# Layer 1's queries and keys of a two-layer encoder: split into bf16 thirds before the transposition instead of after it, and transposed by DMAs, with a new set of ranks

## The chip, the core and the metric

The kernel runs on one core of a Trainium2 chip. The metric is the device time of one execution in microseconds (us). The kernel before was timed in three runs: 1556.82, 1558.4 and 1560.14 us, median 1558.4 us. The five engines run side by side and are named as in the profile: PE (TensorE, matmuls), DVE (VectorE), ACT (ScalarE), POOL (GpSimd) and SP (SyncE, which issues nearly all DMAs, in order).

## What is computed

Two encoder layers over x of 16 sequences, 512 tokens and 128 features, all in fp32, each with a residual and a normalisation without weights ahead of it:

```
x = x + L0_attn(layernorm(x))        # 16 heads of 8 features, biases on q, k, v
x = x + L0_ffn(layernorm(x))         # gated, hidden 384
x = x + L1_attn(layernorm(x))        # q = rms_norm(q) * qn_w, k = rms_norm(k) * kn_w, per head
x = x + L1_ffn(layernorm(x))         # base matmul plus gated low-rank experts

# both attentions, per sequence and head:
softmax((q @ k.T) / sqrt(8)) @ v
```

What matters for the change is layer 1's attention. Its q and k are normalised per head over their 8 features (`rms_norm`) and multiplied by a weight per feature (`qn_w`, `kn_w`), before the scores are formed.

## The kernel before, in words

**Units and tiles.** A unit is the attention of one sequence in one layer, with the feed-forward part behind it: 32 units, numbered n. The order is six units of layer 0, then layer 1 and layer 0 in turn, and six units of layer 1 at the end. A sequence lies in SBUF as 128 partitions by 4 blocks of 128 features ("tokens' rows"); after a transposition it is 128 features by 512 tokens ("features' rows").

**Scores in bf16 thirds.** An fp32 query is split into three bf16 parts that add up to it, and so is a key. Of the nine products six are formed at once: the parts are stacked along the contraction, six slots of 8 features for each head (`QPART`, `KPART`), in the tiles `qst` and `kst`, which exist three times (NST). One more slot, MSLOT, holds the row's maximum, itself split in three, so that the second product comes out with the maximum subtracted. The stacks are filled by DMAs, six copies for each tensor of a unit (L606), and for queries one more that clears MSLOT (L595).

**The three streams of a unit.** `maxima` forms all scores a first time (L777), pair by pair of 512 columns in PSUM, and DVE reduces each pair to the negated row maximum (L790). POOL splits a group's maxima (L813 to L820), a transposing DMA turns them (L824) and another puts them into the query stack (L827). `scores` forms the scores a second time, transposed (L847), and ACT takes the exponential (L861) into a ring of eight buffers. `values` multiplies by the values in fp32 into the bank `acc` (L878); ACT empties it (L895) into one of two `av` buffers, and SP stores that to DRAM (L901).

**Before and behind them.** `pre(n)` normalises the unit's input, transposes it (L548), and makes q, k and v. In layer 0, q and k come straight out of a product in features' rows. In layer 1 they come in tokens' rows (L656), since the norm of each head is a sum over 8 neighbours there: DVE adds the bias and sums squares, POOL runs three Newton steps for the inverse root (L695 to L701) and multiplies (L708, two halves). Then, for keys and for queries:

- PE transposes the four 128x128 blocks of the tensor, in fp32, into one PSUM bank (L726).
- `split_stack` (L560): ACT reads the bank twice, multiplying by the column of norm weights `qkn`, once into an fp32 tile t (L568) and once into the first bf16 third a1 (L570). POOL forms t - a1 (L575), rounds it to the second third a2 (L581), and forms the last one a3 (L585). For the first EARLY units DVE does this instead.
- SP issues the copies of a1, a2 and a3 into the stack (L606), each as soon as its third is there and the slot of unit n - 3 is free.

`post(n)` loads the weighted values and the denominators back (L944 to L956), multiplies by their inverse (L958), projects, and runs the feed-forward part.

**What sets the order.** The program is straight-line: `Plan` simulates the engines while the kernel is written, and picks for each engine what comes next. Each generator yields (engine, duration, rank, kind, what it waits for), and for a DMA also a pair of time until it lands and time that it occupies the DMA engines. On PE a score weighs kinds, ranks and the backlog of DVE and ACT (`choose`, L154); on the others the lowest rank wins among those that can start soon. The constants at the top (LEAD, VLAG, PAIR, AHEAD, UM, UB, LATE, PRE0, PRELEN, POST0, POSTLEN and so on) set the ranks and the booked times. LEAD is how many steps (16 steps to a unit) the maxima run ahead of the scores; PRE0 and PRELEN, POST0 and POSTLEN place the work of `pre` and `post` in steps. On the chip each engine runs its list in the order that was fixed this way, and each instruction waits for what it depends on; an instruction that waits holds up those behind it on its engine.

Of the kernel before, what the change touches and what calls it, by code (L numbers as in the profile page):

```python
# [10 lines left out]
F32 = mybir.dt.float32  # L11
BF16 = mybir.dt.bfloat16
# [36 lines left out]
LEAD = 20  # L49
NP = 8  # L50
VLAG = 3.35
# [19 lines left out]
SAME = 0.05  # L71
PRE0 = 0.03
PRELEN = 20.84
POST0 = 2.81
POSTLEN = 11.82
# [14 lines left out]
def act(n, ptr=0):  # L90
    return 51 + n / 1.2 + 93 * ptr


def dve(n):
    return 55 + n / 0.96
# [212 lines left out]
def encoder_kernel(ctx: ExitStack, tc: tile.TileContext, x, wf, wi, lb, cols, rows, out):  # L308
# [30 lines left out]
    r_t = ring("t", [P, S])  # L339
    r_qk = ring("qks", [P, C, 256], bufs=1)  # L340
# [51 lines left out]
    nc.vector.memset(busy.bitcast(F32), ONES)  # L392
    zero = const.tile([P, S], F32, name="zero")
# [5 lines left out]
    qkn = const.tile([P, 2], F32, name="qkn")  # L399
# [54 lines left out]
    def weights():  # L454
# [6 lines left out]
        nc.vector.tensor_scalar(qkn, cl[:, 2:4], math.sqrt(HD), None, ALU.mult)  # L461
# [12 lines left out]
        at["row2"] = t  # L474
        for k in range(3):
# [84 lines left out]
    def split_stack(pt, b, own, n, qk, layer, nm, tp, pr):  # L560

        if layer == 0:
            arg = dict(bias=cl[:, qk : qk + 1])
        else:
            arg = dict(scale=qkn[:, qk : qk + 1])
# [20 lines left out]
        r_t.give(kt, t)  # L586
        dst = (qst, kst)[qk][n % NST]
        part = (a1, a2, a3)
        avail = (ta, t2, t)
        stack = dst.rearrange("(x k) t s -> k x t s", k=8)  # L590
        end = t
# [17 lines left out]
        for rg, k in zip(r_a, (k1, k2, k3)):  # L609
            rg.give(k, end)  # L610
# [11 lines left out]
    def pre(n):  # L622
# [23 lines left out]
        if layer:  # L646
# [67 lines left out]
            r_ri.give(kri, t)  # L714
        for qk in (1, 0):
            if layer == 0:
                t = yield "PE", 860, pr(), "x", (tT, "w", banks.one, safe, r_t, r_a[0])
                b, pt = banks.take1()
                lo = (WQ0, WK0)[qk]
                product(pt, w[:, lo : lo + P], xT)  # L720
                tp = t
            else:
                tp = yield "PE", 440, pr(), "w", (t, banks.one, safe, r_t, r_a[0])
                b, pt = banks.take1()
                for c in range(C):
                    nc.tensor.transpose(  # L726
                        pt[:, c * P : (c + 1) * P], qk_sb[:, c, qk * P : (qk + 1) * P], ident
                    )
# [3 lines left out]
            plan.spawn(  # L732
                split_stack(pt, b, own, n, qk, layer, f"{qk}{nm}", tp, ramp(pr(), pr() + 3, 8))
            )
# [570 lines left out]
```

## Time and profile before

| | |
|---|---|
| profiled execution: its own time | 1556.45 us |
| its span, first to last instruction | 1554.7 us |
| mean granted TensorE clock | 0.998 |
| L790, DVE reduction of a pair, x1024 | 1208.7 us busy, 1217 ns each |
| L861, ACT exponential of a pair, x1024 | 1017.3 us, 1026 ns |
| L878, PE weighted values, x4096 | 546.6 us, 606 ns |
| L847 and L777, PE scores, x2048 each | 391.0 and 384.7 us, 382 and 381 ns |
| L726, PE transposes of layer 1's q and k, x128 | 21.3 us, 287 and 279 ns |
| L568 and L570, ACT evictions of layer 1's q and k, x64 | 44.1 us |
| L708, POOL normalisation, x32 | 40.2 us, 1276 ns |
| DMA engines, queue q1 (SP's) | 119.02 MB, 28.2% of 16 engines |

How to read it: times of matmuls are modelled and overlap, so a row's busy time on PE is more than the time that PE would save without it; the distance from one start to the next is the better measure. Share of the chain means the chain of work that ended last, followed back from the last instruction to what released it at each step. A wait is written "who, line <- what ended it: total us, times, longest". DMA issues are not counted as busy time of an engine; SP's queue shows for each how long the issue held it.

### The profile page before, as it was taken

The page shows a single profiled execution, that of the slowest core. Times are in us where ns is not written, and L with a number is a line of the kernel's source. Part 1 is how long each engine was busy: PE and PEld are TensorE (multiplying, and loading weights), DVE is VectorE, ACT ScalarE, POOL GpSimd, SP SyncE. Part 2 cuts the span into 40 slices and gives each one's busy share as a digit, 9 for nine tenths or more (in the row PEclk, how much of TensorE's full clock was granted, in tenths as well). Part 3 has the DMA queues.
Part 4 walks back from the last instruction along what each step waited for, and adds up shares of the span by engine and source line. Part 5 has one row for each costly group of instructions (what it writes and reads, how often), then busy time and mean ns, then how long its engine had stood idle before and what let it go on. Part 6 is the DMA issues. An engine that isn't in the chain of part 4 may idle for free.

```text
span 1554.7 us, 38057 instructions
## 1 busy us (share of the span) xinstructions
PE 1492.8 (96%) x14857; PEld 511.5 (33%) x14863; DVE 1453.6 (94%) x1941; ACT 1253.6 (81%) x1506; POOL 833.8 (54%) x1154
## 2 busy tenths in 40 slices
PE   8799999999999999999999999999999999999998
PEld 3222333333333323333333333323333332333223
DVE  6899999999999999999999999999999999999974
ACT  2688878888888888888888888888888888887784
POOL 5634346464464654737556473754647757475122
PEclk9999999999999999999999999999999999999999
DMA  5232223312333132333313333322333213233111
GB/s 138 65 97 72 61 66 89 84 45 75 85 104 83 57 93 69 98 82 98 84 48 84 87 98 83 82 76 66 91 84 92 81 48 85 81 90 97 47 54 39
DMA packets 133220, 122.83 MB, mean 79 GB/s; under 512 B 38660, under 2 KB 108388, under 8 KB 133040
## 3 DMA queue, kind: packets, MB, share of 16 engines
q1 hardware_dynamic: 132032, 119.02, 28.2%
q8 instruction: 116, 1.90, 0.5%
q10 hardware_dynamic: 1008, 1.38, 0.4%
q14 instruction: 64, 0.52, 0.1%
HBM read 23.43 MB, written 38.53 MB: 40 GB/s over the span
## 4 chain that ended last, share of the span: by engine, by line
PE 59%; DVE 25%; ACT 5%; issue 4%; POOL 3%; DMA 2%; SPq 1%; DVEq 0%; POOLq 0%; ACTq 0%
DVE nm L790 22%; PE acc L878 20%; PE pp L847 12%; PE pp L777 11%; PE one L450 10%; ACT p L861 3%; PE one L548 1%; PE one L1057 1%; PE acc L441 1%; PE one L726 1%; DMA rdb<-drd 1%; PE one L1043 1%; SPq L606 1%; ACT th_f L1047 1%; DVE th_f L1049 0%
## 5 line engine op out<-in xcount | busy, mean ns | idle before, releaser
L790 DVE TENSOR_REDUCE nm<-pp 128x2 f32<-128x1024 f32 x1024 | 1208.7, 1217 | 53.2 <-PE pp L777 35.4
L861 ACT ACTIVATE p<-pp 128x1024 f32<-128x1024 f32 x1024 | 1017.3, 1026 | 215.8 <-PE pp L847 193.6
L878 PE MATMUL acc<-p,vst 128*32 128x512 f32 x4096 | 546.6, 606 | 1.0 <-ACT av L895 0.2
L777 PE MATMUL pp<-kst,qst 64*128 64x512 bf16 x2048 | 384.7, 381 | 26.1 <-ACT p L861 11.3
L847 PE MATMUL pp<-qst,kst 64*128 64x512 bf16 x2048 | 391.0, 382 | 19.2 <-DVE nm L790 7.6
L847 PEld LDWEIGHTS <-kst 64*128 64x128 bf16 x2048 | 129.7, 93 | 401.5 <-issue 376.1
L777 PEld LDWEIGHTS <-qst 64*128 64x128 bf16 x2048 | 135.5, 94 | 319.8 <-issue 294.0
L878 PEld LDWEIGHTS acc<-p,vst 128*32 128x32 f32 x4096 | 83.4, 108 | 144.4 <-issue 130.1
L958 POOL TENSOR_TENSOR num<-num,rdb 128x512 f32<-128x512 f32 x31 | 39.5, 1275 | 116.7 <-DMA rdb<-drd 111.9
L895 ACT ACTIVATE av<-acc 128x512 f32<-128x512 f32 x128 | 77.1, 602 | 16.8 <-PE acc L878 14.9
L813 POOL CAST mp<-nm 128x32 bf16<-128x32 f32 x62 | 13.1, 211 | 138.8 <-DVE nm L790 138.8
L1068 POOL TENSOR_TENSOR h_f<-th_f,ub_f 128x512 f32<-128x512 f32 x32 | 40.8, 1276 | 82.9 <-ACT ub_f L1065 77.5
L450 PE MATMUL one<-w,xTa 128*32 128x128 f32 (+1 forms) x1392 | 63.2, 314 | 0.0
L556 POOL TENSOR_TENSOR xt<-xt,row 128x512 f32<-128x512 f32 x48 | 61.4, 1280 | 1.2 <-DVE xnf L510 1.2
L669 POOL TENSOR_TENSOR sq0a<-qksa 128x512 f32<-128x512 f32 x16 | 16.7, 1041 | 80.7 <-DVE qksa L663 61.4
L450 PE MATMUL one<-wd,h_f 128*32 128x128 f32 x1536 | 52.9, 276 | 0.3 <-DVE h_f L1072 0.3
L575 POOL TENSOR_TENSOR t1a<-t1a,a11a 128x512 f32<-128x512 f32 x31 | 36.0, 1161 | 21.3 <-ACT a11a L570 21.3
L450 PEld LDWEIGHTS one<-w,xTa 128*32 128x32 f32 x1392 | 36.9, 109 | 29.1 <-issue 17.1
L450 PEld LDWEIGHTS one<-wd,h_f 128*32 128x32 f32 x1536 | 38.7, 109 | 17.1 <-issue 15.2
L575 POOL TENSOR_TENSOR t0a<-t0a,a10a 128x512 f32<-128x512 f32 x31 | 36.0, 1160 | 10.3 <-ACT a10a L570 8.4
L708 POOL TENSOR_TENSOR qksa<-qksa,ria 128x512 f32<-128x512 f32 x32 | 40.2, 1276 | 1.3
L581 POOL TENSOR_TENSOR a21a<-t1a,zero 128x512 bf16<-128x512 f32 x31 | 39.6, 1277 | 2.4
(176 smaller groups left out, 1540.4 us busy)
## 6 DMA issues: line engine op xcount, KB each, us to landing
dav<-av SPq DMA_DIRECT2D x127, 256.0 KB
kst<-a11a SPq DMA_DIRECT2D x96, 128.0 KB
qst<-a10a SPq DMA_DIRECT2D x93, 128.0 KB
kst<-a21a SPq DMA_DIRECT2D x64, 128.0 KB
qst<-a20a SPq DMA_DIRECT2D x62, 128.0 KB
num<-dav SPq DMA_DIRECT2D x31, 256.0 KB
rdb<-drd SPq DMA_DIRECT2D x31, 256.0 KB
xt<-in_x_dram SPq DMA_DIRECT2D x16, 256.0 KB
```

Of the source, the lines that this page charges most:

```text
L450: nc.tensor.matmul(out[js], lhs[:, js], rhs, start=start, stop=stop, tile_position=(0, 32 * j))
L556: nc.gpsimd.tensor_tensor(xt, xt, row[:, None, lo : lo + P].to_broadcast([P, C, P]), ALU.add)
L575: eng.tensor_tensor(tt, tt, a1, ALU.subtract)
L581: nc.gpsimd.tensor_tensor(a2, tt, zero, ALU.add)
L708: nc.gpsimd.tensor_tensor(qkv4[:, gs], qkv4[:, gs], ri[:, gs, None, :].to_broadcast([P, 8, HD, 8]), ALU.mult,)
L777: nc.tensor.matmul(pt[:, k], qst[n % NST][band, t, qc * P : (qc + 1) * P], kst[n % NST][band, t], start=True, stop=True,)
L790: nc.vector.tensor_reduce(nm[:, :, t % T, qc] if half1 != half else nm[:, half, t % T, qc : qc + 2], pt, AX.X, ALU.max, negate=True,)
L847: nc.tensor.matmul(pair[:, half], kst[n % NST][band, t, kc * P : (kc + 1) * P], qst[n % NST][band, t], start=True, stop=True,)
L861: nc.scalar.activation(pt, pair, AF.Exp, scale=SCALE)
L878: nc.tensor.matmul(acc[32 * j : 32 * j + 32], vst[n % NST][:, kc, lo : lo + 32], p_of[n, i, kc, j // 2][0][:, j % 2], start=(kc == 0), sto ...
L895: nc.scalar.activation(av, acc, AF.Copy)
L1068: nc.gpsimd.tensor_tensor(h[:, f], th, ub, ALU.mult)
```

## The change

In layer 1, q and k stay in tokens' rows until they are in thirds. The norm weights become a row: a matrix of ones is multiplied by a diagonal of `qn_w * kn_w`, once at the start, so that every partition holds their product times 8, and POOL multiplies the queries by it (the keys are left as they are; the scores are the same). `split_tokens` then splits: ACT copies the tensor to the first bf16 third, POOL forms the remainder, rounds it to the second third (by adding zero) and forms the third one. Each third, 128 partitions by 512 bf16, is brought to features' rows by one transposing DMA on SP's queue. The stacking copies follow as before, now in `put_stack`. The PE transposes (L726), the two ACT evictions with scale and the PSUM bank they took are gone, and so is the rank that held this PE work back in layer 1 (`safe`). Layer 0 goes through `split_rows`, which is the old code. A ring of two buffers for each of the three thirds in tokens' rows is new. Nearly all ranks are set anew; EARLY is 2, so that unit 1 is split on DVE as well, and its first normalisation ends there.

```diff
-LEAD = 20
+LEAD = 19
-VLAG = 3.35
+VLAG = 2.04
...
-EARLY = 1
-MAXPR = 4.43
+EARLY = 2
+MAXPR = 9.8
-PAIR = 93.67
+PAIR = 13.08
+TRANS = (3000, 500)
-AHEAD = 447
+AHEAD = 555
-UM = {"m": 1.05, "e": 1.02, "v": 0.0, "x": -0.15, "w": -0.1}
-UB = {"m": 1652, "e": 1199}
-LATE = 10.81
-LATE_M = 7.9
-SAME = 0.05
-PRE0 = 0.03
+UM = {"m": 1.05, "e": 1.02, "v": 0.0, "x": -0.32, "w": -0.29}
+UB = {"m": 1660, "e": 1199}
+LATE = 7.7
+LATE_M = 2
+SAME = 0.02
+PRE0 = 3.16
-POST0 = 2.81
-POSTLEN = 11.82
+POST0 = 4.77
+POSTLEN = 20
...
+    r_b = [ring(f"b{k}", [P, C, P], BF16) for k in (1, 2, 3)]
...
-        nc.vector.tensor_scalar(qkn, cl[:, 2:4], math.sqrt(HD), None, ALU.mult)
...
+        t = yield "DVE", 300, -30, None, (r_rt, r_rt)
+        diag, kb = r_rt.take("diag")
+        nc.vector.tensor_scalar(diag, ident, cl[:, 2:3], cl[:, 3:4], ALU.mult, ALU.mult)
+        t = yield "PE", 224, -30, "x", (t, banks.one)
+        b, pt = banks.take1()
+        product(pt[:, :P], ones, diag)
+        r_rt.give(kb, t)
+        t = yield "DVE", dve(P), -30, None, (t,)
+        nc.vector.tensor_scalar(qkn, pt[:, :P], float(HD), None, ALU.mult)
...
+    def split_tokens(qk_sb, kq, n, qk, nm, t, pr):
+        x = qk_sb[:, :, qk * P : (qk + 1) * P]
+        z4 = zero.rearrange("p (c d) -> p c d", c=C)
+        parts, ks, avail = [], [], []
+        for k in range(3):
+            if k == 0:
+                t = yield "ACT", act(S), pr(), None, (t, r_b[0])
+                bt, kb = r_b[0].take(f"b0{nm}")
+                nc.scalar.activation(bt, x, AF.Copy)
+            else:
+                t = yield "POOL", 1180, pr(), None, (t, (r_t, r_b[2])[k - 1])
+                last = bt
+                if k == 1:
+                    tt, kt = r_t.take(f"t{nm}")
+                    tt = tt.rearrange("p (c d) -> p c d", c=C)
+                    nc.gpsimd.tensor_tensor(tt, x, last, ALU.subtract)
...
+                    nc.gpsimd.tensor_tensor(bt, tt, z4, ALU.add)
+                else:
...
+                    nc.gpsimd.tensor_tensor(bt, tt, last, ALU.subtract)
...
+            e = yield "SP", 600, pr(0.2), None, (t, r_a[k]), TRANS
+            a, ka = r_a[k].take(f"a{k}{nm}")
+            nc.sync.dma_start_transpose(
+                a.rearrange("p (c s) -> p c s", c=C), bt.rearrange("p c d -> p (c d)")
+            )
+            parts.append(a)
+            ks.append(ka)
+            avail.append(e)
+        r_b[2].give(kb, e)
+        yield from put_stack(parts, ks, avail, n, qk, pr)
...
+        if layer:
+            t = yield "POOL", 1280, pr(), None, (t - 80, "qkn")
+            q3 = qk_sb[:, :, :P]
+            nc.gpsimd.tensor_tensor(q3, q3, qkn[:, None, :].to_broadcast([P, C, P]), ALU.mult)
+            kq = [kq, 2]
         for qk in (1, 0):
-            if layer == 0:
-                t = yield "PE", 860, pr(), "x", (tT, "w", banks.one, safe, r_t, r_a[0])
...
-            else:
-                tp = yield "PE", 440, pr(), "w", (t, banks.one, safe, r_t, r_a[0])
-                b, pt = banks.take1()
-                for c in range(C):
-                    nc.tensor.transpose(
-                        pt[:, c * P : (c + 1) * P], qk_sb[:, c, qk * P : (qk + 1) * P], ident
-                    )
-                if qk == 0:
-                    r_qk.give(kq, tp)
+            ends = ramp(pr(), pr() + 3, 8)
+            if layer:
+                plan.spawn(split_tokens(qk_sb, kq, n, qk, f"{qk}{nm}", t, ends))
+                continue
+            t = yield "PE", 860, pr(), "x", (tT, "w", banks.one, safe, r_t, r_a[0])
```

More of the change, by code (lines that the diff above doesn't have):

```diff
@@ L392, in encoder_kernel @@
     nc.vector.memset(busy.bitcast(F32), ONES)
+    ones = const.tile([P, P], F32, name="ones")
+    nc.gpsimd.memset(ones, 1.0)
     zero = const.tile([P, S], F32, name="zero")
@@ L398, in encoder_kernel @@
     wd = const.tile([P, NF, P], F32, name="wd")
[L399 removed]
+    qkn = const.tile([P, P], F32, name="qkn")
     qst = [const.tile([P, 8, S], BF16, name=f"qst{i}") for i in range(NST)]
@@ L474, in weights @@
         at["row2"] = t
+        t = yield "DVE", 300, -30, None, (r_rt, r_rt)
[7 more added lines that the diff above has]
+        nc.vector.tensor_scalar(qkn, pt[:, :P], float(HD), None, ALU.mult)
+        banks.give(b, t)
+        at["qkn"] = t
         for k in range(3):
@@ L558, in add_row, with split_rows @@
         )
-    def split_stack(pt, b, own, n, qk, layer, nm, tp, pr):
-        if layer == 0:
-            arg = dict(bias=cl[:, qk : qk + 1])
-        else:
-            arg = dict(scale=qkn[:, qk : qk + 1])
+    def split_rows(pt, b, own, n, qk, nm, tp, pr):
+        arg = dict(bias=cl[:, qk : qk + 1])
         t = yield "ACT", act(S, 1), pr(), None, (tp,)
@@ L586, in split_stack, with put_stack @@
         r_t.give(kt, t)
+        yield from put_stack((a1, a2, a3), (k1, k2, k3), (ta, t2, t), n, qk, pr)
+    def split_tokens(qk_sb, kq, n, qk, nm, t, pr):
[14 more added lines that the diff above has]
+                    nc.gpsimd.tensor_tensor(tt, x, last, ALU.subtract)
+                    r_b[0].give(kb, max(e, t))
+                    kq[1] -= 1
+                    if kq[1] == 0:
+                        r_qk.give(kq[0], t)
+                    t = yield "POOL", 1180, pr(), None, (t - 80, r_b[1])
+                    bt, kb = r_b[1].take(f"b1{nm}")
+                    nc.gpsimd.tensor_tensor(bt, tt, z4, ALU.add)
+                else:
+                    k1, t1 = kb, t
+                    bt, kb = r_b[2].take(f"b2{nm}")
+                    nc.gpsimd.tensor_tensor(bt, tt, last, ALU.subtract)
+                    r_b[1].give(k1, max(e, t1))
+                    r_t.give(kt, t)
+            e = yield "SP", 600, pr(0.2), None, (t, r_a[k]), TRANS
[8 more added lines that the diff above has]
+        yield from put_stack(parts, ks, avail, n, qk, pr)
+    def put_stack(part, ks, avail, n, qk, pr):
         dst = (qst, kst)[qk][n % NST]
-        part = (a1, a2, a3)
-        avail = (ta, t2, t)
         stack = dst.rearrange("(x k) t s -> k x t s", k=8)
-        end = t
+        end = avail[2]
         if qk == 0 and n >= NST:
@@ L608, in split_stack @@
         at["qk"[qk], n] = end
-        for rg, k in zip(r_a, (k1, k2, k3)):
+        for rg, k in zip(r_a, ks):
             rg.give(k, end)
@@ L714, in pre @@
             r_ri.give(kri, t)
-        for qk in (1, 0):
-            if layer == 0:
-                t = yield "PE", 860, pr(), "x", (tT, "w", banks.one, safe, r_t, r_a[0])
-                b, pt = banks.take1()
[L719 to L722, printed above, removed]
-                tp = yield "PE", 440, pr(), "w", (t, banks.one, safe, r_t, r_a[0])
-                b, pt = banks.take1()
-                for c in range(C):
-                    nc.tensor.transpose(
-                        pt[:, c * P : (c + 1) * P], qk_sb[:, c, qk * P : (qk + 1) * P], ident
-                    )
-                if qk == 0:
-                    r_qk.give(kq, tp)
+        if layer:
[3 more added lines that the diff above has]
+            kq = [kq, 2]
+        for qk in (1, 0):
+            ends = ramp(pr(), pr() + 3, 8)
[3 more added lines that the diff above has]
+            t = yield "PE", 860, pr(), "x", (tT, "w", banks.one, safe, r_t, r_a[0])
+            b, pt = banks.take1()
+            lo = (WQ0, WK0)[qk]
+            product(pt, w[:, lo : lo + P], xT)
             own = r_t.take(f"t{qk}{nm}"), r_a[0].take(f"a1{qk}{nm}")
-            plan.spawn(
-                split_stack(pt, b, own, n, qk, layer, f"{qk}{nm}", tp, ramp(pr(), pr() + 3, 8))
-            )
+            plan.spawn(split_rows(pt, b, own, n, qk, f"{qk}{nm}", t, ends))
         wlo = WQKV1 + 256 if layer else WV0
```

## The prediction

> **What bounds the kernel now.** I read the busy totals first, then the chain that ended last, then the waits of each engine, then one stretch of the steady part instruction by instruction.
>
> ```profile
> PE 1492.8 (96%) x14857; PEld 511.5 (33%) x14863; DVE 1453.6 (94%) x1941; ACT 1253.6 (81%) x1506; POOL 833.8 (54%) x1154
> ```
>
> ```profile
> PE 59%; DVE 25%; ACT 5%; issue 4%; POOL 3%; DMA 2%; SPq 1%; DVEq 0%; POOLq 0%; ACTq 0%
> ```
>
> ```profile
> by line: DVE nm L790 22.0%; PE acc L878 20.1%; PE pp L847 12.1%; PE pp L777 10.8%; PE one L450 10.0%; issue 4.1%; ACT p L861 3.3%; PE one L548 1.4%; PE one L1057 1.3%; PE acc L441 0.9%; PE one L726 0.8%; DMA rdb<-drd 0.8%; PE one L1043 0.7%
> ```
>
> The first line is the page's part 1, the second the chain by engine, the third the chain by line as the chain query prints it. Two engines are nearly full: PE (96%) and DVE (94%), and the chain passes between them, 59% on PE and 25% on DVE. POOL, SP and the DMA engines have room, and the change moves work from PE and ACT to these three. The granted clock is 0.998, so no clock effect has to be weighed. The last line names the one group that the change removes from PE: L726, 0.8% of the chain.
>
> The seven stretches from 540 to 1188 us (648 us, seven pairs of a layer 0 and a layer 1 unit, some 92.5 us each) add up to PE 633.6 us and DVE 624.1 us busy. DVE's idle time there is 23.9 us. In the stretch 380 to 1200 us its largest wait is this one:
>
> ```profile
> DVE nm L790 <- PE pp L777: 15.0, 46, 0.5
> ```
>
> (us in total, times, longest). Scaled to 648 us that is 11.9 us: half of DVE's idle time is a wait for PE, the rest lies between instructions. So time taken from PE can reach the end, up to 11.9 us in these seven pairs; below 648 - 11.9 = 636 us DVE itself is the bound.
>
> **Removed: the transposes on PE (L726).** Around 907 us the PE timeline reads:
>
> ```profile
> 907.31 0.39 PE L777 MATMUL pp<-kst,qst 64*128 64x512 bf16 x2
> 907.63 0.66 PE L726 MATMUL one<-ident,qksa 128*128 128x128 f32 x4
> 908.21 1.07 PE L878 MATMUL acc<-p,vst 128*32 128x512 f32 x8
> ```
>
> Columns: start, length, engine, line, operation. From the start of the four transposes to the next group's start are 0.58 us; the 0.66 is a modelled end that overlaps the next group. Without them L878 would start at 907.63. A layer 1 unit has two such groups, and there are 16 such units: 32 x 0.58 = 18.6 us of PE's time. That is the most that can come back. What of it lay on the path is the chain's share: 0.8% of 1554.7 = 12.4 us. By window it agrees: 0.9% of the 820 us from 380 to 1200 and 1.3% of the 280 us from 1200 to 1480 are 7.4 + 3.6 = 11.0 us, and the units before 380 us bring the rest. Term: **-12.4** (bounds -18.6 and 0). Next late is DVE: seven layer 1 units give 7 x 12.4/16 = 5.4 us, which leaves 642.6 of 648, still above DVE's 636.
>
> **Removed: evictions on ACT (L568, L570).** A layer 1 unit loses four 128x512 activations that read PSUM with a pointer scale (682 to 706 ns, say 689) and gains two copies from SBUF. The nearest row for the copy is L551, 599 ns, whose source is PSUM. So 64 x 0.689 - 32 x 0.599 = 24.9 us less on ACT. ACT is not full (81%), and PE waits for it little: "PE pp L777 <- ACT p L861" 11.3 us and "PE pp L847 <- ACT p L861" 2.5 us in the whole span. ACT's work falls by 24.9 of 1253.6, 2%; but pairs of 1.38 us, in which no exponential runs, become single 0.6 us pieces. Two PSUM banks per unit are also no longer taken. Term: **-1** (0 to -3).
>
> **Added on POOL: the norm weights (one 128x512 multiply).** L708 does the same for two halves in 1.276 us each: 16 x 1.28 = 20.5 us. The three splits per tensor stay on POOL at their durations (1.16, 1.28, 1.16). POOL is 54% busy; its share of the chain is 3% of 1554.7 = 47 us against 834 us busy, so 5.6% of its work lay on the path, and 20.5 x 0.056 = 1.1. Term: **+1** (0, all hidden, to +20.5, none hidden).
>
> **Added on SP and the DMA engines: six transposing DMAs per layer 1 unit,** each 128x512 in bf16, three per tensor; each stacking copy (L606) now waits for its transpose to land. Behind that wait on SP are the stores of the weighted values (L901), the transposes of the maxima (L824, L827) and the denominators' DMAs (L944 to L956). The trace has a transposing DMA of a quarter of this size:
>
> ```profile
> L824 SPq DMA_TRANSPOSE msb<-mp x62: 1102/1137/2137, 93.3 to 1506.9; - x62
> ```
>
> ```profile
> L827 SPq DMA_DIRECT2D qst<-msb x66: 612/635/681, 39.0 to 1509.4; - x66
> ```
>
> ```profile
> L606 SPq DMA_DIRECT2D kst<-a11a x96: 538/596/2050, 13.6 to 1414.1; - x96
> ```
>
> ```profile
> SPq L901 <- ACT av L895: 521.8, 90, 12.5
> ```
>
> Three rows give min/median/max ns on SP's queue, the last a wait. Four times the bytes does not lengthen a plain issue (32 KB 0.635, 128 KB 0.596). For the transpose the bounds are 1.14 us (size is free) and 4 x 1.137 = 4.55 us (all of it grows). I take the middle reading, that only what a transpose costs beyond a plain issue grows: 0.60 + 4 x 0.54 = 2.75 us, and for landing 2.34 us (876.48 to 878.82, L824's issue to its follower's) + 1.6 = 3.95 us. The planner books 0.6 and 3.0 us, so SP runs some 2.15 us late for each. Its issues add up to some 36 us of a 92 us pair; 6 x 2.75 = 16.5 brings them to 53, and SP's longest wait is 521.8 us spent on ACT. The covers: the maxima of a group finish 11.5 steps (33 us) before their scores, and stores of av come every 11.6 us into two buffers, 23.2 us. Six times 2.15 = 13 us fits in both. Term: **0**; if that cover is gone, see the slower rival.
>
> The Trainium skill speaks against this step. "VectorE: DVE Perf Modes", section "Rules for kernel authors", would have a 128x128 transpose on TensorE when PSUM is an acceptable destination and the crossbar DMA only otherwise, and its section "The three transpose paths" has 390 ns against 1309 ns. The trace agrees on the order (0.58 us for four on PE, 1.14 us of SP's queue for one). By that rule, eight blocks at 390 ns for 24 at 1309 would be a loss of 28 us per unit, if the DMA lay on the path. The trace says PE is full and SP is not, so I price by the path.
>
> **Moved at the head.** EARLY = 2 puts unit 1's normalisation and splits on DVE: by unit 0's rows 1.12 + 2 x (0.69 + 0.43 + 0.69) = 4.7 us. DVE stood 4.67 us before L482 at 19.4 to 24.1 us, so part is free, and POOL's later start (28.2 us) is gone. **+2** (0 to 4.7). The weights' row costs one product and two small DVE instructions before the first unit needs them, each below 0.3 us: **+0.5** (0 to 1).
>
> **Ranks.** No row prices a new order. PE's idle time in the steady part is 14.4 of 648 us; I allow half of it, 1.1%, as 7 us either way over the seven pairs, and take **0**.
>
> **Sum:** -12.4 - 1 + 1 + 2 + 0.5 = -9.9. The profiled execution took 1556.45 us (span 1554.7, 1.75 around it): 1546.55. The median of the runs shown, 1558.4, is 1.95 above that execution, so I predict **1548.5**, 0.6% faster.
>
> **Rivals.** *DVE takes over.* The reductions keep their distances, and freed PE time turns into waits of L777 for a free pair. For it: DVE is at 624 + 12 of 648. Against it: its waits for PE have 11.9 us to give. Then a third of 12.4 comes back, and the head and POOL take 3.5: some -1, 1557.
>
> *All of it comes back.* 18.6 + 3 on ACT less 3.5: -18, 1540. For it: freed banks and ACT. Against it: DVE's floor.
>
> *Slower: SP holds the stores.* If a transpose costs near 4.55 us on SP and 6.5 us until it lands, and each copy waits, then a run of three transposes and six copies holds SP 3 x 6.5 + 6 x 0.6 = 23.1 us. The two av buffers cover 23.2 less 2.3 for issue and landing of a store, 20.9 us. From there L895 cannot empty acc and L878 stands: 2.2 us per run, 32 runs, 70 us if every run overruns, 35 if one of each unit does, and a third of that, +23, if the planner's other work breaks most runs. With the -9.9: +13, 1571; the point is about 4 us per issue. For it: the planner books 0.6 where even the small one takes 1.14. Against it: SP's 521.8 us of waiting.
>
> **Chances.** Forecast 0.45 (its own range 1541 to 1555), DVE takes over 0.18 (half of it faster by over 0.2%, half within), all of it 0.07, slower 0.30. Some 0.2%, 3 us, is what a measurement here can tell. Faster 0.45 + 0.09 + 0.07 = 0.61, same 0.09, slower 0.30. The range 1540 to 1576 leaves out half of the third case and about half of the slower one.
>
> **What would show it.** L726 gone from PE and L568/L570 down by half; PE busy lower by up to 21 us (its modelled L726 sum); DVE's wait for L777 below 35.4 us; ACT near 1229; POOL near 854 less the head's 10. The new DMA_TRANSPOSE rows on SP give the price: 1.1 to 2.75 us for the forecast, over 4 for the slower rival, with ACT av waiting for DMA dav. L790 unchanged at 1217 ns. I am wrong if DVE's waits do not shrink, or if PE begins to wait for stacked queries and keys at L777.

## The result and the profile after

The changed kernel is slower. Nine runs of it have a median of 1563.46 us (1560.86 to 1568.3), nine runs of the kernel before on the same chip 1557.57 us; the ratio is 1.0038 with an interval of 1.0025 to 1.0051, so 0.4% or 5.9 us slower. I had forecast 1548.5, 0.6% faster. The sign is wrong.

The profiled execution took 1560.86 us, its span is 1559.1 us, the granted clock 0.999. In the changed kernel the lines are numbered anew: L826 forms the maxima's scores (L777 before), L839 reduces them (L790), L896 forms the second scores (L847), L910 is the exponential (L861), L927 the weighted values (L878), L950 their store (L901), L659 the stacking copies (L606), L873 and L876 the two DMAs of the maxima (L824, L827), L1005 and L1007 the inverse denominators and their multiplication (L956, L958), L454 the shared product helper (L450). New is L632, the transposing DMAs.

The busy totals of the kernel after, the first line of the page's part 1:

```profile
PE 1483.5 (95%) x14745; PEld 502.0 (32%) x14752; DVE 1453.5 (93%) x1952; ACT 1233.9 (79%) x1474; POOL 844.3 (54%) x1163
```

What was to be shed has been shed: PE 9.3 us less, ACT 19.7 less, POOL 10.5 more, and the span is 4.4 us longer all the same. So the loss is not a sum of work; it is waiting. The chain that ended last, by line:

```profile
by line: DVE nm L839 22.0%; PE acc L927 20.3%; PE pp L896 12.0%; PE pp L826 10.6%; PE one L454 8.7%; issue 5.1%; ACT p L910 3.8%; PE one L1092 1.5%; PE acc L445 1.3%; DMA xt<-in_x_dram 1.3%; PE one L1106 1.1%; DMA dav<-av 0.6%; DMA msb<-mp 
```

The 0.8% of the transposes is gone, but "issue" has grown from 4.1 to 5.1%, and the chain runs through other DMAs than before, one of them `msb<-mp`, the maxima on their way into the query stack. The waits say who stands for it (us in total, times, longest). First two lines of the kernel before, then three of the kernel after:

```profile
DVE nm L790 <- PE pp L777: 35.4, 98, 1.2
...
PEld L847 <- DMA qst<-msb: 0.7, 2, 0.5
```

```profile
DVE nm L839 <- PE pp L826: 45.4, 115, 2.1
...
PEld L896 <- DMA qst<-msb: 10.2, 8, 2.6
PE pp L896 <- DMA qst<-msb: 6.1, 4, 2.2
```

DVE's wait for PE did not shrink, it grew from 35.4 to 45.4 us. And the second scores now wait for the maxima in the stack, both the products (PE) and, overlapping with them, their weight loads (PEld); in the kernel before, the only such wait was 0.7 us in two places. The price of the new transposes on SP's queue, min/median/max in ns, for one of the six tiles:

```profile
L632 SPq DMA_TRANSPOSE a01a<-b01a x16: 1207/1254/2148, 257.9 to 1422.4; - x16
```

The medians of the six are 1.19 to 1.31 us: about twice what the planner books (0.6), and less than half of the 2.75 us that I had taken.

**When the time is lost.** The start of each unit's first reduction, worked out of the instructions' start times in the two traces, after less before: -1.6 us at unit 14, -1.5 at unit 20, -1.0 at unit 24, then +1.7 at unit 26, +2.7 at 28, +5.8 at 30, +7.0 at 31, and +4.4 at the end. So three facts have to be explained: a head start of some 2 us, a steady part of layer pairs in which nothing is won (92.5 us per pair before, 92.7 after, from unit 10 to unit 24), and a loss of 8 us in the last six units, which are all of layer 1.

The SP timeline of that last part shows the third fact. A group of maxima is ready (POOL's last instruction for it ended at 1299.40 us). Columns: start, length, queue and line, operation.

```profile
1297.90 1.23 SPq L632 DMA_TRANSPOSE a20a<-b20a  x1
1299.17 0.62 SPq L648 DMA_DIRECT2D qst<-zero  x1
1299.84 1.88 SPq L659 DMA_DIRECT2D qst<-a00a  x3
1301.82 1.20 SPq L873 DMA_TRANSPOSE msb<-mp  x1
1303.06 2.43 SPq L659 DMA_DIRECT2D qst<-a10a  x2
1305.53 0.60 SPq L659 DMA_DIRECT2D qst<-a20a  x1
1306.34 0.62 SPq L876 DMA_DIRECT2D qst<-msb  x1
```

SP stands nowhere for long; it is packed. The maxima's transpose goes out 2.4 us after it could, then three stacking copies pass ahead of its second DMA, which goes out at 1306.34. The same group in the kernel before has the queue to itself:

```profile
1296.31 0.33 SPq L901 DMA_DIRECT2D dav<-av  x1
1298.24 1.15 SPq L824 DMA_TRANSPOSE msb<-mp  x1
1300.54 0.65 SPq L827 DMA_DIRECT2D qst<-msb  x1
1305.71 0.34 SPq L901 DMA_DIRECT2D dav<-av  x1
```

2.3 us between the two DMAs there, 4.5 us here. And PE, in the kernel after:

```profile
1305.34 0.39 PE L826 MATMUL pp<-kst,qst 64*128 64x512 bf16 x2
1305.75 0.39 PE L896 MATMUL pp<-qst,kst 64*128 64x512 bf16 x2
1308.34 0.39 PE L896 MATMUL pp<-qst,kst 64*128 64x512 bf16 x2 [2.20 <-DMA qst<-msb]
```

The bracket holds idle time and what ended it: 2.20 us without a product. (The kernel before stands 1.29 us at about the same place, for a reduction.) Two more gaps behind the maxima, of 1.65 and 1.60 us, are at 1355.9 and 1432.1 us. The margin explains why it happens here. From the last reduction of a group to its first second score are 19 to 21 us in the steady part before and 14 to 17 after; in the last six units they are 7 to 17 us before and 6 to 11 after. Of the twelve groups there, the second DMA of four is now issued 7.5 to 8.3 us behind the reduction; before, it was one, at 8.0. So less margin, and more late DMAs, meet. The margin alone does not do it: the new ranks with the old split (e2 below) have 7 to 13 us there and lose nothing in these units. (These too are worked out of start times.)

### The profile page after: what moved, and what is told of

It is laid out like the page before. It is cut to its first block, busy times and chain, and to the rows that moved or that the text cites. A ratio compares the mean times of both kernels' runs of the same rounds, so it can differ in the third digit from the quotient of the medians.

```text
span 1559.1 us, 37815 instructions
## 1 busy us (share of the span) xinstructions
PE 1483.5 (95%) x14745; PEld 502.0 (32%) x14752; DVE 1453.5 (93%) x1952; ACT 1233.9 (79%) x1474; POOL 844.3 (54%) x1163
## 4 chain that ended last, share of the span: by engine, by line
PE 57%; DVE 25%; issue 5%; ACT 5%; POOL 3%; DMA 3%; SPq 1%; DVEq 0%; POOLq 0%; ACTq 0%
DVE nm L839 22%; PE acc L927 20%; PE pp L896 12%; PE pp L826 11%; PE one L454 9%; ACT p L910 4%; PE one L1092 1%; PE acc L445 1%; DMA xt<-in_x_dram 1%; PE one L1106 1%; DMA dav<-av 1%; DMA msb<-mp 1%; PE one L562 0%; POOL qksa L761 0%; PE pp L454 0%
## 5 line engine op out<-in xcount | busy, mean ns | idle before, releaser
L839 DVE TENSOR_REDUCE nm<-pp 128x2 f32<-128x1024 f32 x1024 | 1202.8, 1216 | 58.3 <-PE pp L826 45.4
L910 ACT ACTIVATE p<-pp 128x1024 f32<-128x1024 f32 x1024 | 1017.3, 1025 | 222.3 <-PE pp L896 180.9
L927 PE MATMUL acc<-p,vst 128*32 128x512 f32 x4096 | 547.4, 604 | 1.6 <-ACT av L944 0.4
L896 PE MATMUL pp<-qst,kst 64*128 64x512 bf16 x2048 | 391.1, 382 | 35.0 <-DVE nm L839 14.9
L826 PE MATMUL pp<-kst,qst 64*128 64x512 bf16 x2048 | 385.2, 380 | 26.9 <-ACT p L910 13.1
L896 PEld LDWEIGHTS <-kst 64*128 64x128 bf16 x2048 | 135.3, 93 | 438.5 <-issue 397.9
L826 PEld LDWEIGHTS <-qst 64*128 64x128 bf16 x2048 | 134.3, 93 | 319.5 <-issue 293.6
L927 PEld LDWEIGHTS acc<-p,vst 128*32 128x32 f32 x4096 | 82.2, 108 | 144.8 <-issue 130.3
L944 ACT ACTIVATE av<-acc 128x512 f32<-128x512 f32 x128 | 77.0, 601 | 16.0 <-PE acc L927 11.4
L518 POOL TENSOR_SCALAR rsf<-mvf 128x4 f32<-128x4 f32 x32 | 7.3, 229 | 120.7 <-DVE mvf L514 120.7
L454 PE MATMUL one<-w,xTa 128*32 128x128 f32 (+1 forms) x1488 | 66.7, 312 | 0.2 <-ACT a10a L581 0.2
L1007 POOL TENSOR_TENSOR num<-num,rdb 128x512 f32<-128x512 f32 x31 | 39.6, 1277 | 28.5 <-DMA rdb<-drd 26.1
L454 PE MATMUL one<-wd,h_f 128*32 128x128 f32 x1536 | 53.1, 276 | 0.0
L454 PEld LDWEIGHTS one<-w,xTa 128*32 128x32 f32 x1488 | 38.1, 109 | 23.3 <-issue 13.4
L553 POOL TENSOR_TENSOR x2f<-xTf,x1f 128x512 fp32r<-128x512 f32 x16 | 20.4, 1277 | 45.3 <-ACT xTf L549 45.3
L454 PEld LDWEIGHTS one<-wd,h_f 128*32 128x32 f32 x1536 | 38.9, 109 | 18.0 <-issue 12.1
L445 PE MATMUL acc<-busy 128*128 128x512 bf16 x133 | 35.5, 405 | 2.7 <-DVE busy L394 1.3
```

The source lines that it names most:

```text
L445: nc.tensor.matmul(acc, busy[:, :P], busy, start=True, stop=True)
L454: nc.tensor.matmul(out[js], lhs[:, js], rhs, start=start, stop=stop, tile_position=(0, 32 * j))
L826: nc.tensor.matmul(pt[:, k], qst[n % NST][band, t, qc * P : (qc + 1) * P], kst[n % NST][band, t], start=True, stop=True,)
L839: nc.vector.tensor_reduce(nm[:, :, t % T, qc] if half1 != half else nm[:, half, t % T, qc : qc + 2], pt, AX.X, ALU.max, negate=True,)
L896: nc.tensor.matmul(pair[:, half], kst[n % NST][band, t, kc * P : (kc + 1) * P], qst[n % NST][band, t], start=True, stop=True,)
L910: nc.scalar.activation(pt, pair, AF.Exp, scale=SCALE)
```

## The experiments

Two theories were to be told apart at first. **Order:** the split itself gives back what was forecast, and the new ranks take more. **Queue:** the new DMAs on SP delay other, short DMAs, and the split's gain on PE is eaten by that. Later a third question came up: whether the gain on PE ever existed.

### Which half of the change costs: the split or the ranks

`e1_split_old_ranks` is the kernel after with the ranks of before (TRANS, which only the new code uses, stays):

```diff
-LEAD = 19
-VLAG = 2.04
-EARLY = 2
-MAXPR = 9.8
...
+LEAD = 20
+VLAG = 3.35
+EARLY = 1
+MAXPR = 4.43
...
```

> The new split with the ranks of before. Theory A (DVE's stream of reductions sets the pace, so PE time that is taken away turns idle): the steady part keeps some 92.6 us per pair of units and the time is within 4 us of before, 1554 to 1562 us. Theory B (the split does give time back, the new ranks lose it): 1542 to 1551 us. Theory C (the transposing DMAs and the extra POOL multiply delay the maxima, whatever the ranks): 1561 us or more, with PE waiting for qst<-msb in the last six units.

`e2_old_split_new_ranks` is the reverse: the kernel before with all the new ranks.

> The old split (TensorE transposes, ACT evictions) with the new ranks and EARLY = 2. Theory A: the ranks alone bring the head's 6 us and nothing in the steady part: 1551 to 1560 us. Theory B: the ranks alone cost what the split gave, 1566 to 1580 us. Theory C: without the new work on POOL and SP the last six units are as fast as before: 1550 to 1556 us.

Measured: e1 1602.86 us, ratio 1.0299 (1.0285 to 1.0313), 46 us slower than before. e2 1560.97 us, ratio 1.0029 (1.0017 to 1.004), 4.3 us slower. e1 has theory C's time but not its mark (PE waits only 0.9 us for `qst<-msb`), and e2 lies 1 us above theory A's range. So the new split in the old order is far off, the new ranks are what makes it bearable, and they cost 4.3 us by themselves. Split and ranks together are 5.9 us slower: under the new ranks, the split as a whole is worth 1.0038 less 1.0029, some +1 us, which the two intervals do not tell from nothing. By units it is not flat: from unit 10 to 24 e2 loses 5.5 us on the kernel before, the kernel after 1.7, so there the split gives back 0.54 us per pair of units of the 1.16 us that its two groups of transposes took; and it loses that again in the last six units.

Where e1 loses is seen in its waits:

```profile
DVE xt L1053 <- PE one L454: 33.8, 14, 6.3
PE one L454 <- POOL num L1007: 33.1, 15, 5.3
```

The projection in `post` waits for POOL, and POOL for the inverse denominators, which make two trips through DRAM on SP's queue. Its SP timeline around one of these waits:

```profile
923.38 2.05 SPq L632 DMA_TRANSPOSE a10a<-b10a  x1
925.54 0.52 SPq L1001 DMA_DIRECT2D drd<-den  x1
926.54 1.21 SPq L632 DMA_TRANSPOSE a20a<-b20a  x1
927.81 0.65 SPq L648 DMA_DIRECT2D qst<-zero  x1
928.50 0.59 SPq L659 DMA_DIRECT2D qst<-a00a  x1
929.19 0.55 SPq L1005 DMA_DIRECT2D rdb<-drd  x1
```

The two short DMAs L1001 and L1005 are 3.65 us apart, with a transpose and two copies between them, after a transpose of 2.05 us ahead of the first. (From 550 to 1480 us this distance is 3.4 us on average in e1 and 2.5 in the kernel before.) POOL multiplies at 933.07, and PE has had nothing to do since 930:

```profile
934.38 1.94 PE L454 MATMUL one<-w,num 128*32 128x128 f32 x32 [4.35 <-POOL num L1007]
936.25 0.61 PE L896 MATMUL pp<-qst,kst 64*128 64x512 bf16 x2
...
937.64 1.94 PE L927 MATMUL acc<-p,vst 128*32 128x512 f32 x8
...
940.13 1.07 PE L927 MATMUL acc<-p,vst 128*32 128x512 f32 x8
```

There is more in these lines than the gap: behind it eight products of L927 take 1.94 us instead of 1.07. The next section on the queue comes back to that.

### What is PE's time worth

`e3_transposes_twice` is the kernel before with each transpose issued twice.

```diff
-                for c in range(C):
+                for c in 2 * list(range(C)):
```

> The kernel before with every TensorE transpose of layer 1's q and k issued twice (same result, same order, the planner books nothing for it): 32 more groups of 0.58 us, 18.6 us of PE. Theory A: the reductions wait a little more, +0 to +7 us. Theory B (PE sets the pace): +12 to +18.6 us.

`e12_one_transpose_of_four` takes three quarters of the same work away: one block is transposed, and the evictions read it four times.

```diff
-                for c in range(C):
+                for c in range(1):
...
+        if layer:
+            pt = pt[:, None, :P].to_broadcast([P, C, P])
```

> The kernel before with one TensorE transpose of each four issued and the ACT evictions reading that block four times (so three quarters of layer 1's q and k are wrong): 96 transposes of 0.145 us, 13.9 us, less on PE, same order. If PE time comes back as it costs when added (12.1 of 18.6 us): -9 us, 1546 to 1550 us. If half of it comes back, as in the steady part under the new ranks: -7 us, 1549 to 1552 us. If taking it away gives nothing because DVE follows at once: 1554 to 1558 us.

Measured: e3 1568.74 us, 1.0082 (1.0068 to 1.0096), 12.1 us slower. e12 1556.99 us, 0.9997 (0.9988 to 1.0006). How much of PE's time the two edits move is again the distance from the start of a group to the next group's start. A group of eight in e3 and one of a single transpose in e12:

```profile
911.96 1.09 PE L726 MATMUL one<-ident,qksa 128*128 128x128 f32 x8
912.98 1.07 PE L878 MATMUL acc<-p,vst 128*32 128x512 f32 x8
```

```profile
910.19 0.33 PE L729 MATMUL one<-ident,qksa 128*128 128x128 f32 x1
910.45 1.07 PE L881 MATMUL acc<-p,vst 128*32 128x512 f32 x8
```

Eight take 1.02 us, four 0.58 to 0.59 (medians), one 0.26; over all 32 groups that is 33.2 us in e3, 19.3 in the kernel before and 10.2 in e12. The two expectations had counted every transpose at 0.145 us, 18.6 us more and 13.9 us less; the distances say 13.9 more and 9.2 less. **Adding 13.9 us costs 12.1; taking 9.2 us away returns nothing** (at most 1.9 us by the interval). The chain's 0.8%, 12.4 us, came near the cost of doing the work twice and was no estimate of the return. (One stretch of 3.4 us at half the granted clock, at 219 us in e12's profile, hides at most 1.7 us; behind it, e12's reductions start 2.1 us later than those of the kernel before at unit 8 and at unit 24, and 2.1 to 3.1 us later between them.)

The other engine was then shortened as well, with statistics over half of the features (`bn_stats` over 64 of 128): in the kernel after (`e4_half_statistics`), in the kernel before (`e13_before_half_statistics`) and in e12 (`e14_both_shorter`).

```diff
-            nc.vector.bn_stats(st[:, c], xt[:, c])
+            nc.vector.bn_stats(st[:, c], xt[:, c, : P // 2])
```

> The changed kernel with the normalisations' statistics taken over 64 of the 128 features (this changes the output): 256 instructions of 278 ns become some 67 ns shorter, some 17 us less on DVE, nothing else. Theory A (DVE sets the pace): -8 to -17 us against the changed kernel, so 1546 to 1555 us. Theory B (PE sets it): -0 to -4 us, 1559 to 1563 us.

> The kernel before with the normalisations' statistics over 64 of 128 features (changes the output): some 12 us less on DVE as e4 measured it, same order. If DVE alone paces the steady part of the kernel before: -7 to -12 us, 1545 to 1550 us. If PE and DVE bind together, so that neither gives anything alone: -3 to +1 us, 1554 to 1558 us.

> e12 and e13 together: 13.9 us less on PE and some 12 us less on DVE, in the old order. If PE and DVE bind together: more than the sum of the two alone, -5 to -12 us, 1545 to 1552 us. If DVE alone paces: as e13. If the order's chain of waits through the PSUM pairs sets the pace, not the length of these pieces: -3 to +1 us.

Measured: e4 1.0023 (1.0013 to 1.0033), e13 0.9984 (0.9975 to 0.9992), e14 0.9981 (0.9972 to 0.999). 10 us less of DVE's work (1453.6 to 1443.3 us busy) brings 2 us in the kernel before. With 9.2 us of PE's time gone too it is 2.5 us (1557.27 to 1554.82), no more than can be told from e13. So it is not that each engine alone is covered by the other and both together would give.

The last test makes DVE far from full: the reductions read 448 of 512 columns, in the kernel before (`e17_before_short_reductions`) and after (`e18_after_short_reductions`).

```diff
-            pt,
+            pt[:, :, : S - 64],
```

> The kernel before with each reduction over 448 of the 512 columns of a bank (the last 64 keys are left out of the maxima, which changes rounding and no more): 1024 times some 133 ns less on DVE, 136 us, inside the loop through the PSUM pairs. If that loop holds the pace: -40 to -100 us, down to where PE binds (the shortest spacing of its groups adds up to 580 of 630 us). If the order holds the pace: 0 to -15 us.

> The changed kernel with the same shorter reductions. If the loop through the PSUM pairs swallowed the PE time that the split frees, it shows now that PE binds: 6 to 18 us faster than the kernel before with short reductions. If the new ranks and SP's queue eat it all the same: within 5 us of it or slower.

Measured: e17 1532.94 us, 0.9837 (0.9822 to 0.9851); e18 1539.6 us, 0.9882 (0.9866 to 0.9899). 124 us less in the reductions' row (1208.7 to 1084.7) bring 25 us, which lies between the two ranges expected for e17, and even then the split with its ranks is 6.7 us behind. The stretch 648 to 1108 us of the steady part, in the two kernels (columns: stretch, then us busy and instructions of PE, PEld, DVE, ACT and POOL, the granted clock, the DMA share and GB/s). First e17, then e18:

```profile
648.00:1108.00 460.00, 450.03 (x4634) 155.78 (x4627) 412.57 (x599) 393.25 (x476) 260.27 (x356) 1.00 0.31 83
```

```profile
648.00:1108.00 460.00, 446.76 (x4592) 152.03 (x4595) 411.54 (x599) 385.71 (x467) 267.23 (x361) 1.00 0.34 92
```

PE is at 97.8% in e17 and at 97.1% in e18; DVE is at 90%. PE, not DVE, is the fullest engine there, and still its work without the transposes leaves no shorter time: from unit 8 to unit 24 e17 gains 12.5 us on the kernel before and e18 12.0. What the new ranks alone would do with short reductions was not run (with full ones, e2 loses 3.0 us over these units), so e18 is a test of split and ranks together.

Where PE's saving goes can be read off the distances from the start of each product to the start of the next, in the kernels before and after, from 550 to 1180 us. The products that are neither scores nor values, the transposes among them, take 137.5 us in place of 146.9. Behind the 435 groups of maxima's scores in the same stretch, as many in both, the distance to the next product grows from 134.5 to 140.7 us: of 9.4 us that PE no longer spends on the one, 6.2 stand behind the other. What PE waits for there is in its waits of that stretch, first before, then after:

```profile
PE pp L847 <- DVE nm L790: 0.2, 1, 0.2
```

```profile
PE pp L896 <- DVE nm L839: 5.8, 17, 0.4
```

The second scores now wait for reductions, which hand the pairs of PSUM banks back. In e12 this wait is 2.3 us. DVE's wait for the maxima's scores grows in the same stretch as well, from 11.4 to 18.6 us. So each of the two engines waits longer for the other.

### What the queue costs

`e5_old_ranks_true_issue` is e1 with one number changed, the time that the planner books on SP for a new transpose; `e6_new_ranks_true_issue` is the kernel after with the same edit.

```diff
-            e = yield "SP", 600, pr(0.2), None, (t, r_a[k]), TRANS
+            e = yield "SP", 1250, pr(0.2), None, (t, r_a[k]), TRANS
```

> The new split with the old ranks, but the planner books 1.25 us of SP for a transposing DMA, as it was measured, in place of 0.6. Theory S (the 46 us of the split with the old ranks come from SP's queue, which runs late against a plan that books half of the issue time, so that the denominators' DMAs and with them the weighted values are late): at least half of the 46 us goes, 1556 to 1580 us. Theory P (they come from the longer POOL work of layer 1, or from ranks that place the projection too early whatever is booked): 1585 us or more.

> The changed kernel with 1.25 us of SP booked for a transposing DMA. Theory S: the order gets better where SP is crowded, above all in the six last units, 1554 to 1562 us. Theory P or no connection: 1561 to 1568 us, the planner's order is merely another one.

`e7_old_ranks_new_post` is e1 with only the two ranks of `post` new (POST0 = 4.77, POSTLEN = 20), since e1's waits are in `post`.

> The new split with the old ranks but POST0 and POSTLEN of the change, which place the work behind the attention about two steps (6 us) later and stretch it. Theory S and theory P both have the projection wait for late weighted values, so it gains much: 1556 to 1575 us. If other ranks (PRE0, LEAD, VLAG) are behind the 46 us, it stays over 1585 us.

Measured: e5 1578.78 us, 1.0146 (1.0133 to 1.016), 24 of e1's 46 us are back. e6 1559.93 us, 1.0026 (1.0016 to 1.0036), not to be told from after (1.0025 to 1.0051). e7 1601.99 us, 1.0289 (1.0273 to 1.0305): no help. That the order knows the true length of an issue is worth half of the loss in the old ranks; a later place of `post` alone is worth nothing. From the last store of a unit's weighted values to POOL's multiplication are 15.0 us on average in the kernel before, 17.2 in e1 and 17.6 in e5 (worked out of the start times from 550 to 1480 us): in e5 the path is no shorter, but its order allows for it.

`e16_old_ranks_plain` is e1 with the transposes replaced by plain DMAs of the same bytes, whose issue is as long as the planner believes.

```diff
-            nc.sync.dma_start_transpose(
-                a.rearrange("p (c s) -> p c s", c=C), bt.rearrange("p c d -> p (c d)")
-            )
+            nc.sync.dma_start(a, bt.rearrange("p c d -> p (c d)"))
```

> The new split with the old ranks and plain DMAs of the same size in place of the transposing ones (output changed), so that an issue takes the 0.6 us that the planner books. Theory S: as good as booking the true time or better, 1565 to 1582 us against 1603. If landing or POOL's chain is behind the 46 us: over 1590 us.

`e15_dummy_transposes` puts the queue's load alone into the kernel before: six transposing DMAs per layer 1 unit that nobody reads and the planner does not know.

```diff
+                if layer and which not in done:
+                    done.add(which)
+                    scr, _ = r_scr.take(f"scr{which}{nm}")
+                    nc.sync.dma_start_transpose(
+                        scr.rearrange("p (c s) -> p c s", c=C), part[which]
+                    )
```

> The kernel before with six transposing DMAs per layer 1 unit added: each third of q and k goes once more, transposed, into a scratch tile that nobody reads; the planner books nothing for it. 96 times some 1.25 us of SP's queue. Theory S (SP running late against the plan delays the denominators' DMAs and the maxima): +15 to +40 us. If SP's issues alone are harmless, as the prediction had it: 0 to +4 us.

Measured: e16 1575.66 us, 1.0114 (1.01 to 1.0128), 28 of 46 us back. e15 1567.3 us, 1.006 (1.0045 to 1.0076): 10 us slower, between the two ranges that I had given it. The profile shows no wait for one of these DMAs, so the 10 us come from the load itself, on SP's queue or on the DMA engines. They come in two places, 3.4 us at unit 6 and 8 us at unit 30, and the waits of e15 are those of e1 in small:

```profile
PE one L451 <- POOL num L966: 9.7, 7, 4.6
```

A plain DMA may also land sooner than a transposing one. That this is not what e16 (and e10 below) changes is seen in the waits of SP's queue: in e1 and in the kernel after they hold none for the landing of a new transpose. What is left of e1's loss, 22 us in e5 and 18 in e16, is still in part PE waiting for POOL's multiplication: 33.1 us in e1, 16.2 in e5, 14.1 in e16, 3.4 in the kernel before. Which of the old ranks or of POOL's longer work keeps it there was not tried.

**Gap and clock.** Part of e1's loss is not the gaps themselves. Stretches of e1 around the gap shown above, with the columns as in the table of stretches of e17; the granted clock is the third figure from the right:

```profile
926.00:930.00 4.00, 3.31 (x24) 0.75 (x20) 3.84 (x4) 3.37 (x4) 0.64 (x3) 1.00 0.39 67
930.00:934.30 4.30, 0.03 (x2) 0.00 (x0) 1.58 (x2) 0.62 (x1) 1.23 (x1) 0.84 0.80 201
934.30:936.00 1.70, 1.62 (x32) 1.38 (x32) 0.00 (x0) 0.00 (x0) 0.03 (x1) 0.50 0.65 172
...
940.00:942.00 2.00, 2.00 (x18) 0.45 (x20) 1.38 (x2) 1.46 (x2) 1.92 (x3) 1.00 0.01 4
```

It is 1.00 ahead of the gap, 0.50 behind it, and 1.00 again from 940 us on. The trace's clock records of e1 hold nine such stretches between 100 and 1530 us, of 3.4 or 6.8 us each, 44.4 us together. At half the clock they give away 22.2 us of PE's time. The kernel before and the kernel after have none. Beside it stands PE's idle time between groups, gaps over 0.5 us from 100 us on, from the same traces:

| kernel | idle in gaps, us | clock given away, us | both, more than before | time, more than before |
|---|---|---|---|---|
| before | 8.7 | 0 | | |
| after | 18.6 | 0 | 9.9 | 5.9 |
| e1 old ranks | 43.6 | 22.2 | 57.1 | 46.2 |
| e5 with the true issue | 29.3 | 5.1 | 25.7 | 22.3 |
| e16 plain DMAs | 25.4 | 5.1 | 21.8 | 18.4 |
| e15 dummies | 16.2 | 6.8 | 14.3 | 10.0 |
| e8 (below) | 11.4 | 0 | 2.7 | -0.7 |

Gaps and clock follow the loss in every row, 3 to 11 us above it; in e1, 7.0 of the 44.4 us lie inside gaps, so 3.5 us are counted twice. So e1's 46 us go with gaps and, around the gaps, the halved clock; of the 24 us that e5 returns, up to 17 are clock. That the clock's share is additive is argued from the sums, not shown by a run of its own.

The Trainium skill bears on this: "TensorE: Matmul & The Clock Gate", section "Part 1: The HAM clock gate", describes a clock that falls to half after an idle window of about 3.4 us and returns after a busy one. The halves and the lengths of 3.4 and 6.8 us agree. The gap that it takes was shorter here: in e1 a gap of 1.23 us ahead of 837.09 us, after one of 0.74 us at 834.5, was followed by 3.4 us at half clock, and in e16 a gap of 2.16 us; at 1028.5 us in e1 three gaps of 0.5 to 0.7 us within 3 us were enough. In the kernel after a gap of 2.20 us was not followed by it, and in e11 (below) one of 2.44 us was not.

### The last six units

Three edits take load off the path from POOL over SP to the query stack, in the part where the kernel after loses its 8 us. `e8_tail_on_tensore` uses the old way (transposes on PE, two evictions on ACT) from unit 26 on, with the weight multiplication left on POOL; `e9_tail_and_true_issue` adds the booking of 1250 ns.

```diff
-            if layer:
+            if layer and n < 26:
                 plan.spawn(split_tokens(qk_sb, kq, n, qk, f"{qk}{nm}", t, ends))
                 continue
```

> The changed kernel with TensorE transposes (and two ACT evictions each) again for the last six units, all of layer 1; the weights' multiply stays on POOL. Theory C (the last six units lose some 5.7 us because the transposing DMAs and stacking copies crowd SP ahead of the maxima's DMAs): -4 to -8 us against the changed kernel, 1554 to 1559 us, and PE's waits for qst<-msb go. If the loss there comes from POOL's multiply or from the order as such: 1561 to 1566 us.

> The last two helpful edits together: TensorE transposes for the last six units, and 1.25 us of SP booked for each transposing DMA before them. If the two gains (7.6 and 2 us against the changed kernel) add up: 1551 to 1555 us, ahead of both kernels. If the booking only helped the last six units: 1555 to 1558 us.

`e10_plain_copies` is the kernel after with plain DMAs, as in e16; `e11_no_weight_multiply` the kernel after without POOL's multiplication by the weights:

```diff
-            nc.gpsimd.tensor_tensor(q3, q3, qkn[:, None, :].to_broadcast([P, C, P]), ALU.mult)
```

> The changed kernel with a plain DMA of the same 128 KB in place of each transposing one, in the same order (q and k then stay in tokens' rows, which changes the output). A plain issue takes 0.6 us of SP, not 1.2. Theory S (the loss is SP's queue): the waits for qst<-msb in the last six units shrink and the time falls by 2 to 6 us against the changed kernel, 1557 to 1561 us. If landing or the order sets it: 1562 to 1566 us.

> The changed kernel without POOL's multiply by the norm weights (it is left out, so the weights are missing from the output): 16 times 1.28 us less on POOL, in the same order. If POOL's longer chain delays the maxima in the last six units: -3 to -6 us against the changed kernel, 1557 to 1560 us. Theory S: 0 to -2 us.

Measured: e8 1555.81 us, 0.9998 (0.9989 to 1.0006); e9 1556.61, 1.0 (0.9991 to 1.0009); e10 1555.9, 0.9998 (0.999 to 1.0007); e11 1555.03, 0.999 (0.9979 to 1.0). e8, e10 and e11 each bring back the time of before, 6 to 8 us less than after (each against the kernel before on its own chip), and the true booking adds nothing to e8. The waits for the maxima go with it in two of the three. Of PE's 6.1 us (PEld's 10.2) in the kernel after, 0.2 (2.8) are left in e10, and in e8 one line:

```profile
PEld L906 <- DMA qst<-msb: 1.3, 2, 0.9
```

In e11, 3.3 us (6.2) are left. The start of unit 31's first reduction, 7.0 us behind the kernel before in the kernel after, is 4.2 us ahead of it in e8, 0.9 behind in e10 and 2.6 behind in e11. The tail's loss is thus shown to be the maxima's way through a packed SP: it goes with the transposes' longer issue (e10) and with the transposes themselves (e8). POOL's later hand-over has a part in it (e11); the rest of e11's gain lies outside these waits and stays open. The three gains do not add up: each takes away the same loss. e8 is level with the kernel before and not ahead of it; no version that was tried beats both kernels beyond what a measurement can tell, but for those that leave DVE's or POOL's work out.

## Why the prediction was wrong, step by step

- **Removed on PE, -12.4: failed, and it is the main step.** "What of it lay on the path is the chain's share: 0.8%". That took the chain's share for the return of taking the work away. Doubling it cost 12.1 us (e3, 13.9 us added); taking 9.2 us of it away returned 0 (e12). I had checked the next limit against DVE's busy sum (636 of 648 us) and found 11.9 us of room; e14 and e17 show that DVE's sum is not the next limit either. The two engines run in a fixed order and hand each other pairs of PSUM banks; the saved time turns up behind the maxima's scores, where the second scores wait for reductions (5.8 us from 550 to 1180 us, before 0.2). What in the order holds the pace of 92.5 us per pair stays open: 10 us less on DVE, 9.2 us less on PE, and both together take at most 2.5 us off the whole time, and a tenth less of the reductions 1.6 us off each pair.
- **Removed on ACT, -1.** 19.7 us less busy, near the count of 24.9. The copy takes 628 ns where I took 599. No run shows its own effect.
- **Added on POOL, +1: undersized.** The duration was right (1275 ns), the price was not: without the multiplication the kernel after is as fast as before, some 7.5 us faster than with it (e11). A mean share of the chain hid that the last six units have no cover for it.
- **SP, 0: failed.** The duration was overestimated (2.75, measured 1.2 to 1.3), the price underestimated. I compared the queue's total and the cover of the two av buffers, and took 33 us as the maxima's cover from a constant of the planner. The trace has 20 us in the steady part and 7 to 17 in the last six units; in the kernel after, with 6 to 11 us there, the second DMA of four of twelve groups is issued 7.5 to 8.3 us behind the reduction. What SP's queue cost in place of 0: 6 to 7 us in the last six units (e8, e10), and 10 us as a load added to the kernel before (e15).
- **Head, +2 and +0.5: wrong sign, small.** Unit 10's reductions start 2.7 us earlier, 1.1 us earlier with the ranks alone (e2). But e1, which keeps EARLY = 1, starts them 6.3 us earlier, so it is not EARLY that brings it, and no run shows these two terms alone.
- **Ranks, 0: they cost 4.3 us** (e2; 2.6 to 6.2 by its interval), inside the 7 us allowed. Without them the split costs 46 us (e1). The new ranks keep the split from most of that loss.

**The rivals.** "DVE takes over" had PE's gain returning by a third; it returns by nothing under the old ranks and by 0.54 of 1.16 us per pair under the new ones. Its mechanism is there in part: PE does wait longer for reductions, at the second scores rather than at L777. But DVE waits longer for PE as well, and less work on DVE frees little (e14, e17), so DVE is not simply the engine that takes over. "All of it comes back" is out. "SP holds the stores" had the engine and the reason ("the planner books 0.6 where even the small one takes 1.14") but the wrong victim, and so the wrong point: not the stores of av at 4 us per issue, but the short DMAs of maxima and denominators at 1.2. Its sign held; its time, 1571, was 7.5 us too high.

**My marks for being wrong** were the right ones: DVE's waits did not shrink, and PE began to wait for the query stack, at the second scores instead of the first.

## What to carry to other kernels

A share of the chain is not the return of taking the work away (here 12.4 us by the share, 0 measured; adding cost 12.1); in an order fixed by hand between two nearly full engines, test a removal by leaving the work out before paying for its replacement. A DMA issue holds SP's queue: look at who stands behind it, and at the smallest slack of those in the thinnest part of the kernel, not at the queue's total. Book an issue at its true length: under the old ranks that alone returned 24 of 46 us (under the new ones nothing clear). And a gap on PE can cost twice, where the granted clock halves around it, as it did nine times in e1.

## What was not expected of the hardware

- A transposing DMA of 128x512 bf16 holds SP for 1.19 to 1.31 us (medians of the six rows), one of a quarter of the size for 1.16 (L873). The size hardly matters for the issue; in e15, with other sources, it is 1.25 to 1.29 us.
- Around gaps of 1.2 to 5.3 us on PE, and once after three of 0.5 to 0.7 us, the granted clock fell to half for 3.4 or 6.8 us, but not around all of them (2.20 us in the kernel after, 2.44 in e11): eight products of L927 took 1.94 us instead of 1.07, two of L896 0.61 instead of 0.39.
- An ACT copy of 128x512 from SBUF to bf16 takes 628 ns, not less than the 599 ns of a copy out of PSUM.
